# One or two one-element memsets on GpSimd behind each gather, in four stretches of a graph kernel

## The chip, the cores and the metric

The kernel runs on one core of one Trainium2 chip. The metric is the time of one execution on the device in microseconds (us); runs are summed up by their median. The engines are TensorE (PE in the profile, its weight loads PEld), VectorE (DVE), ScalarE (ACT), GpSimd (POOL) and SyncE (SP, which issues most plain DMAs). A profiled execution gives a row for each instruction.

## The reference

12500 nodes with 128 features each and 200000 edges, which are sorted by their target node. Each edge has one of ten relations, the place of the greatest of ten of its attributes. Two layers of the same form follow each other, and then a residual and a normalization:

```python
def _rgcn_layer(x, src, dst, edge_type, w_rel, root, bias):
    N = x.shape[0]
    seg = dst * NUM_REL + edge_type
    xs = x[src]
    sums = jax.ops.segment_sum(xs, seg, num_segments=N * NUM_REL)
    cnt = jax.ops.segment_sum(jnp.ones(seg.shape, x.dtype), seg, num_segments=N * NUM_REL)
    mean = (sums / jnp.maximum(cnt, 1.0)[:, None]).reshape(N, NUM_REL, -1)
    return jnp.einsum('nrd,rdo->no', mean, w_rel) + x @ root + bias

edge_type = jnp.argmax(msg[:, NODE_EMB_DIM:-NODE_EMB_DIM], axis=1).astype(jnp.int32)
h = jax.nn.relu(_rgcn_layer(x, src, dst, edge_type, w_rel1, root1, b1))
g = _rgcn_layer(h, src, dst, edge_type, w_rel2, root2, b2)
out = _layernorm(x + g, axis=-1)
```

All of it is in 32-bit floats.

## The kernel before, in words

The edges are cut into 1563 tiles of 128. For a tile the kernel fetches the 128 source rows with one indirect DMA from GpSimd, which the text calls a gather (`gathered`, line 835; the tile `g`). VectorE builds a one-hot matrix from the targets and relations of the tile's edges, weighted by one over the count (`hots`, line 842; the tile `oh`). TensorE multiplies the two into a bank of PSUM (line 1079 in the first layer, `zp`; line 1620 in the second, `zy` and `zq`), and VectorE adds the bank to the sums of the nodes (line 868 in the first layer, line 1650 in the second; both are named `cc` in the profile).

The first layer (`layer_1`) walks over the tiles in parts of four. The first 177 tiles gather rows of `x`. The other 1386 gather from a table `XH` that holds the input features and, for nodes already done, the first layer's result beside them, 1 KB a row; from these the kernel takes sums for both layers at once. When a block of nodes is complete (`finish`), it is multiplied by the weights of the relations, made into the hidden features, and stored into `XH` and into `YD`, a table of the hidden features times each weight of the second layer.

The second layer (`layer_2`) has two kinds of tiles. 177 of them gather from `YD` for the tiles that had no second half in the first layer (named `YD,idxE`). Then 678 tiles gather from `YD` along a list that is put together on the chip: the edges whose source was not yet known when they were passed (named `YD,idxB`). Between them TensorE multiplies the second layer's stored sums by the weights (line 1533, `alone`), and complete blocks are transposed, added to `x`, normalized and stored (lines 1552 and 775).

Both layers follow an order that is written out by hand, instruction by instruction (`manual_schedule`); each engine works through its own list in order and waits for others by semaphores. On GpSimd this list holds, after some set-up, nothing but gathers: 177 + 1386 + 177 + 678 = 2418. They write into a few buffers in turn, sixteen gathers' worth. Within a buffer the places are filled forwards and backwards by turns, so that in the main the first gather of a group of four carries the wait for TensorE's last reader:

```python
turn = used[id(g)] = 1 - used.get(id(g), 1)
slot = [p % 2 * QB + j if plain else 2 * (QB - 1 - j if turn else j) for j in range(n)]
```

The tile `lane` is a constant of 128 x 128 floats; after lines 361 to 363, which build another constant from it, the kernel does not use it.

Of the kernel before, what the change touches and what calls it, by code (L numbers as in the profile page):

```python
# [31 lines left out]
OB = 7  # L32
GQ = 8
GB2 = 8
AHEAD = 1
BEHIND = 2
LAND = 2
# [33 lines left out]
def rgcn_resnorm_kernel(ctx: ExitStack, tc: tile.TileContext, x, src, dst, attr, w_rel1, root1, b1,  # L71
# [7 lines left out]
    nc = tc.nc  # L79
# [82 lines left out]
    for l, (a, last) in enumerate(((0, SPLIT), (SPLIT, NR))):  # L162
        while a < last:
            b = a + 1
# [9 lines left out]
            a = b  # L174
# [87 lines left out]
    def chunk_rows(c):  # L262
        return min(CT, NT - c * CT)
# [65 lines left out]
    lane = const.tile([P, P], F32, name="lane")  # L329
# [26 lines left out]
    eps = const.tile([P, 1], F32, name="eps")  # L356
    nc.vector.memset(eps, EPS)

    own = const.tile([P, P], F32, name="own")
    first = float(chunk_rows(NCH - 1) * P) - 0.5  # L360
    nc.vector.tensor_scalar(own, lane, first + HALF, None, op0=ALU.is_gt)
# [471 lines left out]
    def gathered(g, j, table, idx, n):  # L833

        nc.gpsimd.indirect_dma_start(out=g[:, j * C:(j + n) * C], out_offset=None, in_=table,  # L835
                                     in_offset=bass.IndirectOffsetOnAxis(ap=idx, axis=0))

    def hots(keys, weights, cols, n, m):

        oh = next_of("oh", hots_)  # L840
        for j in range(n):
            nc.vector.tensor_scalar(oh[:, j * m:(j + 1) * m], cols[:, :m], keys[:, j:j + 1], weights[:, j:j + 1],  # L842
                                    op0=ALU.is_equal, op1=ALU.mult)
        return oh

    def offsets(row, t0, n, limits, ring=True):

        lims = [limits(t0 + j) for j in range(n)]
        if ring:
            laps = [lap_of_tile(t0 + j) * RN for j in range(n)]  # L850
            lims = [(lo - a, hi - a) for (lo, hi), a in zip(lims, laps)]
            assert all(hi + WN <= RW for _, hi in lims)
        vals = nc.values_load_multi_w_load_instructions(  # L853
            row, engines=[DVE], min_val=min(a for a, _ in lims), max_val=max(b for _, b in lims),
            skip_runtime_bounds_check_because="clamped to these nodes on the chip")[1]
        return [nc.s_assert_within(v, a, b, skip_runtime_bounds_check_because="clamped to these nodes on the chip")
                for v, (a, b) in zip(vals, lims)]
# [50 lines left out]
    def layer_1():  # L908
# [135 lines left out]
        fixed = [ps_z.tile([P, YB], F32, name=f"zp{i}") for i in range(4)]  # L1044
        for p in range(-AHEAD, NPT + BEHIND):
            if p + AHEAD < NPT:
                t0, n = parts[p + AHEAD]
                ohs[p + AHEAD] = hots(keyE[:, t0:t0 + n], wE[:, t0:t0 + n], iotaP, n, KW)
            if p < 0:
                continue  # L1050
            t = p * QB
            if p < NPT:
                t0, n = parts[p]
                plain = t0 + n <= NX
                if not plain or p % 2 == 0:
                    g = next_of("g", gathers if plain else gathers[:NEAR])
                if not plain:
                    turn = used[id(g)] = 1 - used.get(id(g), 1)
                slot = [p % 2 * QB + j if plain else 2 * (QB - 1 - j if turn else j) for j in range(n)]
                for j in range(n):  # L1060
                    i = t0 + j
                    idx = idxE[:, i:i + 1]
                    if i < NX:
                        gathered(g, slot[j], x, idx, 1)
                    else:
                        gathered(g, slot[j], XH[:N + limit_of(i)], idx, 2)
                made = (g, ohs.pop(p), slot)
# [67 lines left out]
    for a in range(0, NREL * RW, YB):  # L1135
        m = min(NREL * RW - a, YB)
# [284 lines left out]
    def layer_2():  # L1421
# [156 lines left out]
        for p in range(-AH, NB + BE):  # L1578
# [21 lines left out]
            if p < NB:  # L1600
                second, t0, n, w = bunches[p]
                oh = ohs.pop(p)
                zps[p] = zp = next_of("zp", banks)
                for j in range(n):
                    if made % QB == 0:
                        m = made // QB % NEAR
                        g, first = gathers[m // 2], m % 2 * QB
                        turn = used_[m] = 1 - used_.get(m, 1)
                    at = first + (QB - 1 - made % QB if turn else made % QB)
                    made += 1  # L1610
                    t = t0 + j
                    if second:
                        gathered(g, at, YD[:, :], idxB[:, t:t + 1], 1)
                    else:
                        gathered(g, at, YD[:NREL * (limit_of(t) + 1), :] if t >= T0 else YD[:, :], idxE[:, t:t + 1], 1)
                    gs[j] = g, at
                for j in range(n):
                    g, at = gs.pop(j)
                    o = 0 if second else j * w
                    nc.tensor.matmul(zp[:, o:o + w], g[:, at * C:(at + 1) * C], oh[:, j * w:(j + 1) * w],  # L1620
                                     start=not second or j == 0, stop=not second or j == n - 1)
                    between.run(issued[p] + j + 1)
                i = issued[p + 1]
# [11 lines left out]
            for q in [q for q in sorted(zps) if q <= p - (1 if p >= NB - 4 else BE)]:  # L1635
                second, t0, n, w = bunches[q]
                for j in range(1 if second else n):
                    t = t0 + j
                    if (second, t) not in offs:
                        if second:  # L1640
                            m = min(GB2, (UX if t < UX else NT2) - t)
                            assert {t // P, (t + m - 1) // P} <= ready
                            vals = offsets(rowB[:, t:t + m], t, m, bounds2, False)
                        else:
                            m = min(GB2, (NX if t >= T0 else T0) - t)
                            vals = offsets(rowP[:, t:t + m], t, m, bounds, False)
# [181 lines left out]
```

## Time and profile before

| | |
|---|---|
| Runs | 3640.88 us median of 3 (3640.8 to 3644.05) |
| Profiled execution | 3672.03 us, its span 3670.2 us |
| Granted TensorE clock | 0.753 on average |
| GpSimd | 2287.4 us busy (62%), 2418 gathers of 0.945 us |
| DMA | 529.25 MB, mean 144 GB/s |

A row of a timeline gives the start, the duration, the engine, the line, the operation and the tiles (written <- read), how many instructions the row merges, and in brackets the idle time of the engine before it with what ended it. "issue" is idle time in which the profile shows no wait; "remote" is a wait whose end the profile can't give to an instruction. A row of a group gives busy time and mean duration, then the idle time before the group's instructions, and what ended most of it. Ends of matmuls are modelled. The profiled execution is some 31 us longer than the median of the runs.

### The profile page before, as it was taken

The page shows a single profiled execution, that of the slowest core. Times are in us where ns is not written, and L with a number is a line of the kernel's source. Part 1 is how long each engine was busy: PE and PEld are TensorE (multiplying, and loading weights), DVE is VectorE, ACT ScalarE, POOL GpSimd, SP SyncE. Part 2 cuts the span into 40 slices and gives each one's busy share as a digit, 9 for nine tenths or more (in the row PEclk, how much of TensorE's full clock was granted, in tenths as well). Part 3 has the DMA queues.
Part 4 walks back from the last instruction along what each step waited for, and adds up shares of the span by engine and source line. Part 5 has one row for each costly group of instructions (what it writes and reads, how often), then busy time and mean ns, then how long its engine had stood idle before and what let it go on. Part 6 is the DMA issues. An engine that isn't in the chain of part 4 may idle for free. (4 is left out here: it accounts for less than half of the span.)

```text
span 3670.2 us, 37654 instructions
## 1 busy us (share of the span) xinstructions
PE 2319.0 (63%) x10645; PEld 1779.5 (48%) x10645; DVE 1991.3 (54%) x6410; ACT 511.8 (14%) x799; POOL 2287.4 (62%) x2430
## 2 busy tenths in 40 slices
PE   1557676767676767677666767653566666566444
PEld 0445565555555555565555655543534343333333
DVE  4646476767575757565655656358644232332332
ACT  1111111212121212121212121110000000000000
POOL 5663666666666666666666666556666666666665
PEclk7677787888887888878888878765667777677555
DMA  4553555455555555555555555542334443443222
GB/s 121 159 164 94 187 157 186 151 167 159 177 174 159 189 158 190 158 192 159 190 156 188 159 159 156 147 111 55 105 112 139 129 153 123 148 152 116 61 57 52
DMA packets 345316, 529.25 MB, mean 144 GB/s; under 512 B 55520, under 2 KB 225723, under 8 KB 345100
## 3 DMA queue, kind: packets, MB, share of 16 engines
q0 software_dynamic: 99552, 249.45, 23.9%
q1 hardware_dynamic: 218105, 264.48, 21.7%
q10 hardware_dynamic: 27443, 12.82, 1.2%
q8 instruction: 89, 1.46, 0.2%
q14 instruction: 127, 1.04, 0.1%
HBM read 372.75 MB, written 160.19 MB: 145 GB/s over the span
## 5 line engine op out<-in xcount | busy, mean ns | idle before, releaser
L835 POOL DMA_INDIRECT g<-XH,idxE x1386 | 1309.9, 945 | 769.7 <-issue 368.6
L1079 PEld LDWEIGHTS zp<-oh,g 128*128 128x128 f32 x5898 | 918.4, 234 | 396.5 <-DVE cc L868 180.1
L1079 PE MATMUL zp<-oh,g 128*128 128x120 f32 x5898 | 957.0, 320 | 228.6 <-DVE cc L868 132.3
L868 DVE TENSOR_TENSOR cc<-cc,zp 128x240 f32 (+1 forms) x1563 | 606.5, 388 | 816.1 <-remote 354.1
L835 POOL DMA_INDIRECT g<-YD,idxB x678 | 640.3, 944 | 342.4 <-issue 190.7
L936 PE MATMUL yb<-w,a 128*128 128x512 f32 (+1 forms) x576 | 354.9, 706 | 383.3 <-ACT ys L942 229.0
L842 DVE TENSOR_SCALAR oh<-bank,keyE,wE 128x120 f32<-128x120 f32 x1563 | 517.3, 393 | 0.0
L1620 PEld LDWEIGHTS zy<-oh,g 128*128 128x128 f32 x1168 | 244.8, 275 | 317.9 <-DVE cc L1650 119.1
L1620 PE MATMUL zy<-oh,g 128*128 128x12 f32 (+30 forms) x1168 | 258.4, 347 | 206.5 <-DVE cc L1650 114.6
L942 ACT ACTIVATE ys<-yb 128x512 f32<-128x512 f32 (+2 forms) x291 | 152.8, 525 | 1384.8 <-remote 612.0
L1533 PE MATMUL alone<-cc,w 128*128 128x512 f32 (+1 forms) x440 | 305.3, 782 | 31.6 <-issue 16.9
L936 PEld LDWEIGHTS yb<-w,a 128*128 128x128 f32 x576 | 111.0, 240 | 413.7 <-ACT ys L942 255.9
L828 PE MATMUL pf<-cc,w 128*128 128x256 f32 (+2 forms) x1040 | 254.9, 401 | 25.7 <-issue 13.4
L835 POOL DMA_INDIRECT g<-in_x_dram,idxE x177 | 167.3, 945 | 138.2 <-PE zp L1079 60.0
L828 PEld LDWEIGHTS pf<-cc,w 128*128 128x128 f32 x1040 | 208.4, 215 | 63.9 <-issue 26.0
L835 POOL DMA_INDIRECT g<-YD,idxE x177 | 168.2, 951 | 110.8 <-issue 62.7
L775 DVE TENSOR_TENSOR cc<-pf,x 128x256 f32<-128x256 f32 (+2 forms) x52 | 21.2, 409 | 358.9 <-remote 219.9
L797 ACT ACTIVATE cc<-zero 128x1280 f32<-128x1280 f32 x170 | 214.6, 1262 | 0.0
L1620 PEld LDWEIGHTS zq<-oh,g 128*128 128x128 f32 x542 | 110.8, 253 | 151.2 <-DMA g<-YD,idxB 74.0
L842 DVE TENSOR_SCALAR oh<-columns,keyB,wB 128x45 f32<-128x45 f32 (+35 forms) x678 | 176.8, 335 | 0.0
L1620 PE MATMUL zq<-oh,g 128*128 128x45 f32 (+33 forms) x542 | 122.9, 341 | 84.3 <-DMA g<-YD,idxB 59.5
L1650 DVE TENSOR_TENSOR cc<-cc,zy 128x12 f32 (+24 forms) x306 | 59.0, 193 | 142.6 <-remote 61.0
(265 smaller groups left out, 1528.4 us busy)
## 6 DMA issues: line engine op xcount, KB each, us to landing
cc<-SD SPq DMA_DIRECT2D x21, 2560.0 KB
SD<-cc SPq DMA_DIRECT2D x41, 1280.0 KB
YD<-ys SPq DMA_DIRECT2D x194, 256.0 KB
m<-in_edge_attr_dram SPq DMA_DIRECT2D x48, 672.0 KB
g<-XH,idxE POOLq DMA_INDIRECT x1386
YD<-ys SPq DMA_DIRECT2D x97, 128.0 KB
XH<-hb SPq DMA_DIRECT2D x44, 256.0 KB
g<-YD,idxB POOLq DMA_INDIRECT x678
```

Source lines behind the costliest of these rows:

```text
L775: nc.vector.tensor_tensor(v[:p, s], pr[:p, s], xb[:p, s], op=ALU.add)
L797: nc.scalar.activation(cc[:, l, h * H:(h + 1) * H, o:o + n], zero[:, None, :n].to_broadcast([P, H, n]), AF.Copy)
L828: nc.tensor.matmul(po[:, :n], wsb[l][:, r, :], sums[:, r], start=(r == 0), stop=(w is None and r == NREL - 1))
L835: nc.gpsimd.indirect_dma_start(out=g[:, j * C:(j + n) * C], out_offset=None, in_=table, in_offset=bass.IndirectOffsetOnAxis(ap=idx, axis=0))
L842: nc.vector.tensor_scalar(oh[:, j * m:(j + 1) * m], cols[:, :m], keys[:, j:j + 1], weights[:, j:j + 1], op0=ALU.is_equal, op1=ALU.mult)
L868: nc.vector.tensor_tensor(s, s, z, op=ALU.add)
L936: nc.tensor.matmul(yb[:h, :m], fin_a[k][:, b * P:b * P + h], wsb[1][:, r:r + m // C, :], start=True, stop=True)
L942: nc.scalar.activation(ys[:h, :m], yb[:h, :m], AF.Copy)
L1079: nc.tensor.matmul(zp[:, o + l * KW:o + (l + 1) * KW], g[:, (slot[j] + l) * C:(slot[j] + l + 1) * C], oh[:, j * KW:(j + 1) * KW], start=Tr ...
L1533: nc.tensor.matmul(po[:, :n], wsb[1][:, r, :], sds[j][:, r, :n], start=(r == 0), stop=(r == NREL - 1))
L1620: nc.tensor.matmul(zp[:, o:o + w], g[:, at * C:(at + 1) * C], oh[:, j * w:(j + 1) * w], start=not second or j == 0, stop=not second or j = ...
L1650: nc.vector.tensor_tensor(s, s, zps[q][:, j * w:(j + 1) * w], op=ALU.add)
```

## The change

A table of four stretches is added, in numbers of the gather in the order in which the program issues them, with one or two memsets for each gather of the stretch. The memset writes zero to one element of `lane`. A counter of gathers runs along while the program is built. Gathers 400 to 799 and 1740 to 1999 get one memset each, gathers 800 to 1199 and 2000 to 2199 get two; all others get none. Numbers 400 to 1199 lie in the first layer (all of them gathers from `XH`); number 1740 is the first gather along the list that is put together on the chip.

```diff
+SPACED = ((400, 800, 1), (800, 1200, 2), (1740, 2000, 1), (2000, 2200, 2))
...
+    pause = lane[:1, :1]
+    number = [0]
...
         nc.gpsimd.indirect_dma_start(out=g[:, j * C:(j + n) * C], out_offset=None, in_=table,
                                      in_offset=bass.IndirectOffsetOnAxis(ap=idx, axis=0))
+        for a, b, m in SPACED:
+            if a <= number[0] < b:
+                for _ in range(m):
+                    nc.gpsimd.memset(pause, 0.0)
+        number[0] += 1
```

## The prediction

> **What bounds the kernel now.** I read the page first (engine shares), then the gathers' rows in the four stretches that get memsets, then the order of time inside a few runs of gathers.
>
> ```profile
> span 3670.2 us, 37654 instructions
> ...
> PE 2319.0 (63%) x10645; PEld 1779.5 (48%) x10645; DVE 1991.3 (54%) x6410; ACT 511.8 (14%) x799; POOL 2287.4 (62%) x2430
> ```
>
> No engine is full: each of them waits more than a third of the time. So the question is what a gather waits for. Gathers are numbered from 0 in the order in which they are issued. Numbers 400, 800 and 1200 start at 645.46, 1246.88 and 1836.99 us, numbers 1740, 2000 and 2200 at 2666.74, 3050.01 and 3336.52 us; these starts cut out the four stretches. In the table by stage (stretch, its length, busy time and count of line 835) and in the groups of GpSimd in the same four windows (busy, mean ns | idle before, and what ended it):
>
> ```profile
> 645.46:1246.88 601.42, 378.18 (x400) 0.82 0.54 168
> 1246.88:1836.99 590.11, 377.96 (x400) 0.83 0.55 174
> 2666.74:3050.01 383.27, 245.67 (x260) 0.74 0.41 130
> 3050.01:3336.52 286.51, 188.87 (x200) 0.73 0.47 148
> ...
> L835 POOL DMA_INDIRECT g<-XH,idxE x400 | 378.2, 945 | 221.3 <-issue 107.4 <-remote 54.3 <-PE zp L1079 49.9
> L835 POOL DMA_INDIRECT g<-XH,idxE x400 | 378.0, 945 | 213.1 <-issue 107.7 <-remote 53.2 <-PE zp L1079 42.3
> L835 POOL DMA_INDIRECT g<-YD,idxB x260 | 245.7, 945 | 137.6 <-issue 71.2 <-remote 34.6 <-PE zy L1620 21.7
> L835 POOL DMA_INDIRECT g<-YD,idxB x200 | 188.9, 944 | 97.6 <-issue 55.5 <-remote 28.1 <-PE zq L1620 8.0
> ```
>
> A gather keeps GpSimd 0.945 us, and the next one starts 0.30 us after it even when nothing is waited for (rows below): 1.25 us from start to start. The stretches take 1.50, 1.48, 1.47 and 1.43 us per gather (length by count). The rest is waiting. With 0.30 us per gather taken off the idle time, it is 221.3 - 120 = 101.3, 213.1 - 120 = 93.1, 137.6 - 78 = 59.6 and 97.6 - 60 = 37.6 us, or 0.253, 0.233, 0.229 and 0.188 us per gather. That is the room into which the memsets go.
>
> How the room lies is seen in order of time. Twelve gathers of the first layer and sixteen of the second, each with the wait that closes the run (last number in the brackets: idle before):
>
> ```profile
> 1199.46 0.95 POOL L835 DMA_INDIRECT g<-XH,idxE  x1 [2.33 <-PE zp L1079]
> ...
> 1217.30 0.94 POOL L835 DMA_INDIRECT g<-XH,idxE  x1 [3.15 <-PE zp L1079]
> 1218.55 0.94 POOL L835 DMA_INDIRECT g<-XH,idxE  x1 [0.30 <-issue]
> ...
> 1231.05 0.95 POOL L835 DMA_INDIRECT g<-XH,idxE  x1 [0.30 <-issue]
> 1234.85 0.95 POOL L835 DMA_INDIRECT g<-XH,idxE  x1 [2.86 <-remote]
> ...
> 2806.01 0.94 POOL L835 DMA_INDIRECT g<-YD,idxB  x1 [3.32 <-PE zy L1620]
> ...
> 2824.80 0.95 POOL L835 DMA_INDIRECT g<-YD,idxB  x1 [0.30 <-issue]
> 2829.07 0.94 POOL L835 DMA_INDIRECT g<-YD,idxB  x1 [3.32 <-remote]
> ```
>
> So GpSimd runs a dozen gathers or so at 1.25 us, stops at the head of a group of four until TensorE has given a buffer back (2.9 to 3.3 us here, the usual 0.30 us included), and runs again: 17.55 us for the twelve, 23.06 us for the sixteen.
>
> The trace holds a small version of the change. Two runs of the same lengths contain a pause of their own (0.81 and 0.52 us where 0.30 is usual):
>
> ```profile
> 1152.03 0.95 POOL L835 DMA_INDIRECT g<-XH,idxE  x1 [1.37 <-PE pf L953]
> ...
> 1162.53 0.94 POOL L835 DMA_INDIRECT g<-XH,idxE  x1 [0.81 <-issue]
> ...
> 1169.76 0.94 POOL L835 DMA_INDIRECT g<-XH,idxE  x1 [2.54 <-PE zp L1079]
> ...
> 2728.19 0.94 POOL L835 DMA_INDIRECT g<-YD,idxB  x1 [2.74 <-PE zy L1620]
> ...
> 2743.43 0.94 POOL L835 DMA_INDIRECT g<-YD,idxB  x1 [0.52 <-issue]
> ...
> 2751.25 0.94 POOL L835 DMA_INDIRECT g<-YD,idxB  x1 [3.14 <-remote]
> ```
>
> With 0.51 us more inside the run the closing wait is 2.54 us, not 2.86 to 3.15, and twelve gathers take 17.73 us against 17.55 (and 17.84 for the run that starts at 1199.46). With 0.22 us more, sixteen take 23.06 us: the same. Time lost inside a run is taken off the wait at its end. What is behind that wait sets the pace, not GpSimd.
>
> **The change part by part.** It adds 400 x 1 + 400 x 2 + 260 x 1 + 200 x 2 = 1860 memsets of one element to GpSimd's queue, each behind a gather and ahead of the next; nothing is removed or moved, no DMA is added, no other engine reads what they write. The line that names the element and the counter cost nothing on the chip: they act while the program is built. A memset's target was last used by VectorE before the first gather, so its wait, if it has one, has long been met; behind it stands the next gather alone, and who waits for that is TensorE.
>
> What one memset costs behind a gather no row shows. The nearest are the memsets with which the program begins:
>
> ```profile
> 0.25 0.10 POOL L1816 MEMSET const-float32-0.0<- 128x1 f32 x1 [0.25 <-issue]
> 0.28 0.10 POOL L1816 MEMSET const-float32-1.0<- 128x1 f32 x1
> 0.31 0.11 POOL L1816 MEMSET const-bfloat16-1.0<- 128x1 bf16 x1
> ```
>
> One lasts 0.10 us, and the next starts 0.03 us behind it. Lower end: nothing (it fits in the 0.30 us gap), or 0.03 us each, 56 us in all. Upper end: the 0.30 us gap comes once more for each, 0.40 us each, 744 us. I take 0.10 us for a memset alone and 0.13 us for a pair (the second 0.03 us behind the first), the rows of the same instruction on the same engine: 40, 52, 26 and 26 us in the four stretches, 144 us in all.
>
> The Trainium skill, Perfetto Trace Analysis, "GPSIMD Engine Instruction", says to time such instructions by the spacing of their starts, not by the span reported; by that rule and the rows above the estimate is 0.03 us each, 12, 24, 8 and 12 us, and the forecast would be the same.
>
> What of the 144 us lies on the path: they stand against 101.3, 93.1, 59.6 and 37.6 us of room, so each stretch has room over, and by the runs with a pause the wait at the end of the run gives it back. Sum: 0 us. If the cover goes, the cost is the surplus per stretch. The break-even is 0.25 us for the single memset in the first stretch and 0.23 us in the third, 0.233 and 0.188 us for the pair in the second and fourth. The fourth is the thinnest, also because there TensorE does wait for gathers: the first fence lists who waited for line 835 in the first stretch, after the dots in the fourth.
>
> ```profile
>   PE yb L936: 14.6, 2
>   PE pf L953: 1.2, 1
> ...
>   PE zy L1620: 19.5, 16
>   PEld zq L1620: 17.7, 19
> ...
>   PE zq L1620: 12.3, 16
> ```
>
> In the first layer 16 us of 601 are waited for gathers; in the fourth stretch about 32 us of 287 on TensorE (19.5 + 12.3). Late gathers there matter only if the run's end no longer absorbs them.
>
> **The rivals.** *Faster: the pauses let signals through.* Late in a run VectorE, ScalarE and GpSimd start together long after TensorE's last matmul; after the last gather of the program a consumer starts at once:
>
> ```profile
> 1506.74 1.05 PE L1079 MATMUL zp<-oh,g 128*128 128x120 f32 x8
> 1512.84 0.84 DVE L868 TENSOR_TENSOR cc<-cc,zp 128x240 f32 x2 [3.47 <-remote]
> 1512.88 0.60 ACT L942 ACTIVATE ys<-yb 128x512 f32<-128x512 f32 x1 [8.38 <-remote]
> 1513.07 0.94 POOL L835 DMA_INDIRECT g<-XH,idxE  x1 [2.13 <-remote]
> ...
> 3655.61 0.45 PE L1552 MATMUL pf<-ident,cc 128*128 128x128 f32 x1 [3.75 <-DVE cc L1650]
> 3656.09 0.29 DVE L775 TENSOR_TENSOR cc<-pf,x 128x128 f32<-128x128 f32 x1 [0.63 <-PE pf L1552]
> ```
>
> From TensorE's end to the others' start it is 1512.84 - 1507.79 = 5.05 us in a run, 0.03 us without gathers. If back-to-back gathers hold TensorE's signals up and a pause frees them, all closing waits could go. At 1.35 and 1.45 us per gather (0.10 us for one, 0.20 for two) the stretches would take 540 + 580 + 351 + 290 = 1761 us against 1861.3: 100 us less at most, 3541 us. Half of it, since TensorE and VectorE have limits of their own: 3590 us. Against it: the pauses of 0.51 and 0.22 us above shortened nothing.
>
> *Slower: a pair costs more than its room.* One mechanism: each memset holds GpSimd for its full time and the second waits for the first. At 0.15 us each the second stretch lacks 120 - 93.1 = 27 us and the fourth 60 - 37.6 = 22 us, the singles nothing: + 49 us, 3690 us. It decides from 0.094 us per memset in the fourth stretch, 0.117 us in the second. For it: 0.10 us is already the row's length. Far end: 0.40 us each against the room lacks 59 + 227 + 44 + 122 = 452 us, 4093 us.
>
> *Slower: nothing is absorbed.* If the closing wait is counted from GpSimd's last gather of a run, every memset adds: 56 us (0.03 each) to 186 us (0.10 each), 3697 to 3827 us. Against it stand the same two runs.
>
> *Slower: the shared port.* VectorE's one-hot rows in the third and fourth stretch take 120.4 us of 669.8 (second row: the gathers of the third stretch, shortest, median and longest in ns):
>
> ```profile
> L842 DVE TENSOR_SCALAR oh<-columns,keyB,wB 128x46 f32<-128x46 f32 (+25 forms) x460 | 120.4, 334 | 0.0
> ...
> L835 POOL DMA_INDIRECT g<-YD,idxB x260: 938/944/1022, 2666.7 to 3048.8; - x130
> ```
>
> A memset that met one of these would wait half of 0.334 us in 18% of cases, 0.03 us on average: 12 us for the 400 memsets of the fourth stretch. With 0.20 us a pair there (40 us) that makes 52 against 37.6: + 14 us, 3655 us. Against it: the longest gather is 78 ns over the median. The Trainium skill, SBUF — State Buffer, "Who interferes with whom", has it that VectorE in a two-port mode and a GpSimd instruction lock each other out of a shared port; no run here shows that wait.
>
> **How the numbers follow.** The profiled execution took 3672.03 us (span 3670.2), 31 us above the median of the runs, 3640.88; I carry differences over to the median. A change under 0.2% (7 us) can't be told from none here.
> - Absorbed, no change: 0.38, 3641 us, with a range of its own from 3633 to 3648.
> - Signals pass, faster: 0.32, about 3590 us, 3541 at most.
> - A pair costs more than its room: 0.15, about 3690 us; with the far end of 0.40 us: 0.05.
> - Nothing absorbed: 0.06, 3697 us and more. The port: 0.04, 3655 us.
>
> The forecast is the likeliest, 3641 us. The range from 3580 to 3695 leaves out the deep half of the faster case's tail (about 0.08) and the far slower cases (about 0.12). Faster 0.32, same 0.38, slower 0.30.
>
> **What would show it.** Right: 1860 memsets on GpSimd's row; start to start 1.28 to 1.35 us with one, 1.28 to 1.4 us with two; closing waits shorter by that much, and the four stretches still about 601, 590, 383 and 287 us long. Wrong to the slow side: a start to start of over 1.44 us with two, no closing waits left, and TensorE's waits for gathers up. Wrong to the fast side: VectorE's and ScalarE's starts follow TensorE within 0.1 us in mid-run, and stretches shorter by tens of us. A stretch without memsets that moves by more than 5 us would be something I have not seen.

## The result, and the profile after

The changed kernel takes 3650.7 us (median) beside 3640.84 us of the kernel before: a ratio of 1.0037, interval 1.0020 to 1.0055, so 7 to 20 us more (the ratio is not that of the two medians, 1.0027; the two can differ by some 0.1%). That is slower by a little, inside the range of 3580 to 3695 us, but outside the 3633 to 3648 us of the case that I held likeliest. The profiled execution took 3649.4 us, at its median; that of before stood 31 us above its own.

Page of the kernel after (span, busy time by engine):

```profile
span 3647.6 us, 39514 instructions
...
PE 2315.0 (63%) x10645; PEld 1770.1 (49%) x10645; DVE 1994.4 (55%) x6410; ACT 512.0 (14%) x799; POOL 2451.8 (67%) x4290
```

4290 - 2430 = 1860 instructions more on GpSimd. The same four stretches (gathers 400, 800, 1740 and 2000 onward) of the kernel after, by windows with GpSimd's busy time in line 838 alone:

```profile
636.55:1234.01 597.46, 378.24 (x401) 0.81 0.54 169
1234.01:1826.18 592.17, 377.87 (x401) 0.82 0.56 173
2649.68:3026.70 377.02, 246.00 (x261) 0.74 0.42 133
3026.70:3321.46 294.76, 188.77 (x201) 0.76 0.46 144
```

Against before (601.42, 590.11, 383.27, 286.51) the singles' stretches are not longer; the pairs' are, the second by 2 us, which is within the spread shown further down, the fourth by 8 us. The parts without memsets are shorter by 8.9, 6.3 and 7.5 us (up to gather 400, 1200 to 1740, from 2200 on), since before's profiled execution was a long one; so single stretches of these two traces are no fair comparison, and further traces are added below. What a memset does is seen in order of time, GpSimd of the kernel after, first in the third stretch (one), then in the fourth (two):

```profile
2702.18 0.94 POOL L838 DMA_INDIRECT g<-YD,idxB  x1 [2.44 <-remote]
2703.13 0.09 POOL L843 MEMSET lane<- 1x1 f32 x1
2703.43 0.94 POOL L838 DMA_INDIRECT g<-YD,idxB  x1 [0.22 <-issue]
2704.38 0.09 POOL L843 MEMSET lane<- 1x1 f32 x1
2704.68 0.94 POOL L838 DMA_INDIRECT g<-YD,idxB  x1 [0.21 <-issue]
...
3103.46 0.94 POOL L838 DMA_INDIRECT g<-YD,idxB  x1 [0.61 <-issue]
3104.40 0.23 POOL L843 MEMSET lane<- 1x1 f32 x2
3104.79 0.94 POOL L838 DMA_INDIRECT g<-YD,idxB  x1 [0.15 <-issue]
3105.73 0.23 POOL L843 MEMSET lane<- 1x1 f32 x2
3106.11 0.94 POOL L838 DMA_INDIRECT g<-YD,idxB  x1
3107.06 0.23 POOL L843 MEMSET lane<- 1x1 f32 x2
3107.44 0.94 POOL L838 DMA_INDIRECT g<-YD,idxB  x1
3108.39 0.23 POOL L843 MEMSET lane<- 1x1 f32 x2
3109.23 0.94 POOL L838 DMA_INDIRECT g<-YD,idxB  x1 [0.61 <-issue]
```

One memset disappears in the 0.30 us gap: 1.25 us from start to start (2703.43 to 2704.68), as without it. A pair makes it 1.33 us (3103.46 to 3104.79), and once per four gathers 1.79 us (3107.44 to 3109.23): a group of four takes 5.77 us, 1.44 us per gather, with no wait for another engine. That is as much as the fourth stretch had in all. The two memsets of a pair do not overlap: one lasts 0.09 us, the two 0.23 us, so the second starts 0.15 us after the first and 0.06 us after its end (medians of all 600 pairs). In the trace each memset waits for a semaphore that the memset before it raises; both write the same element. The waits fit the slower pace. Who waited for line 838 in the fourth stretch after (the rows of before are in the prediction), then VectorE's waits there, before and after:

```profile
  PEld zy L1628: 70.7, 64
  PE zy L1628: 55.6, 47
  PEld zq L1628: 42.3, 42
  PE zq L1628: 35.5, 30
```

```profile
DVE cc L1650 <- remote: 50.6, 7, 16.3
DVE cc L775 <- remote: 43.4, 4, 15.5
```

```profile
DVE cc L778 <- PE pf L1560: 87.6, 10, 12.7
DVE cc L1658 <- PE zy L1628: 32.2, 14, 5.4
```

TensorE's waits for gathers went from 31.8 to 91.1 us (zy and zq); VectorE's largest waits of before, without a releaser that the profile can name ("remote", the late signals), are gone from this stretch. GpSimd has become the bound of that stretch.

### The profile page after: what moved, and what is told of

Its sections match the earlier page's. It is cut to its first block, busy times and chain, and to the rows that moved or that the text cites. A ratio compares the mean times of both kernels' runs of the same rounds, so it can differ in the third digit from the quotient of the medians.

```text
span 3647.6 us, 39514 instructions
## 1 busy us (share of the span) xinstructions
PE 2315.0 (63%) x10645; PEld 1770.1 (49%) x10645; DVE 1994.4 (55%) x6410; ACT 512.0 (14%) x799; POOL 2451.8 (67%) x4290
## 5 line engine op out<-in xcount | busy, mean ns | idle before, releaser
L1087 PEld LDWEIGHTS zp<-oh,g 128*128 128x128 f32 x5898 | 902.6, 230 | 428.0 <-DVE cc L876 210.8
L843 POOL MEMSET lane<- 1x1 f32 x1860 | 167.3, 90 | 35.4
```

The costliest lines, as they stand in the source:

```text
L843: nc.gpsimd.memset(pause, 0.0)
L1087: nc.tensor.matmul(zp[:, o + l * KW:o + (l + 1) * KW], g[:, (slot[j] + l) * C:(slot[j] + l + 1) * C], oh[:, j * KW:(j + 1) * KW], start=Tr ...
```

## The experiments

Theory, formed from these rows: one memset is free; a pair makes GpSimd's own pace 1.44 us per gather and a little over, of which 0.46 us per group falls on the group's head; a stretch takes the slower of that pace and of what the other engines allow. Rivals: the loss comes from the number of instructions, from every pair, or is the time of the memsets. On two chips the kernel before took 3096 to 3098 us, on a third 3636 to 3640 us. Each kernel is compared with before on its own chip. The first eight ran where before takes 3096 us, the last four where it takes 3640 us.

**One memset behind every gather.**

```
SPACED = ((0, 2418, 1),)
```

> One memset behind each of the 2418 gathers, none a pair. Theory 'price at the head of a group' (in the changed kernel one memset hides in the 0.30 us gap, start to start still 1.25 us; a pair makes it 1.33 us, and 1.79 us at the head of each group of four gathers): no change, 3641 us, within 6; start to start stays 1.25 us, closing waits as before. Rival 'each instruction costs' (the 10 us come from 1860 more instructions, 5.4 ns each, wherever they stand): 3654 us.

Measured: 3110.75 us against 3096.33, 1.0047 (1.0033 to 1.0061), 14 us for 2418 memsets, 0.006 us each. Start to start stays 1.25 us. On this evidence alone "each instruction costs" fits; the next runs refute it.

**Pairs in one layer.**

```
SPACED = ((177, 1563, 2),)      # first layer
SPACED = ((1563, 2418, 2),)     # second layer
```

> Two memsets behind each of the 1386 gathers of the first layer, none elsewhere. Theory 'price at the head': GpSimd's own pace there becomes (3 x 1.33 + 1.79) / 4 = 1.445 us per gather, under the 1.51 us (2088 us for 1386) that the stretch takes: no loss, 3635 to 3647 us; long closing waits gone, and VectorE's waits for late signals much reduced. Rival 'each instruction costs': 3656 us. Rival 'every pair adds its 0.08 us' (nothing absorbed): 3641 + 111 = 3752 us.

> Two memsets behind each of the 855 gathers of the second layer, none elsewhere. Theory 'price at the head': GpSimd's own pace, 1.445 us per gather, is over the 1.433 us that the fourth stretch had, and TensorE waits for gathers as it does in the changed kernel's fourth stretch (1.474 us against 1.433 us): 855 x 0.041 = 35 us, 3676 us (3660 to 3690). Rival 'each instruction costs': 3650 us. Rival 'every pair adds its 0.08 us': 3709 us.

Measured: 3379.77 and 3260.74 us, 1.0917 (1.0902 to 1.0932) and 1.0537 (1.0523 to 1.0551): 283 and 164 us more, 0.20 and 0.19 us per pair. None of my numbers held; they supposed that before takes 3641 us. The group's 5.77 us less four times 1.25, divided by four, is 0.19 us, about this price.

**Where in the group the price falls.** Pairs in the second layer, left out behind the last gather of each group; then there alone:

```
-            if a <= number[0] < b:
+            if a <= number[0] < b and number[0] % 4 != 2:   # and in the other run == 2
```

> As the run with pairs in the second layer, but nothing behind the last gather of each group of four, so that no memset stands right ahead of a group's head. Theory 'price at the head': the 0.46 us per group goes, GpSimd's own pace is (3 x 1.33 + 1.25) / 4 = 1.31 us, and the loss goes with it: 3641 us (3625 to 3648). If the pauses let TensorE's signals through as well, it may be below 3630. Rival 'every memset costs', by number or by time: three quarters of the loss of the run with all pairs, 3667 us if that one is 3676.

> Second layer alone: two memsets behind the last gather of each group of four, so right ahead of the next group's head; nothing behind the other three. Where the kernel before takes 3096 us (no closing waits, GpSimd sets the pace): theory 'price at the head' 0.54 us per group (1.79 - 1.25), 214 groups: +116 us, or +108 by subtraction (164 us with all pairs less 56 without those at the head). Rival 'the delay gathers up over several pairs in a row' (a single pair is no more than its 0.08 us): +17 us. Where the kernel before takes 3641 us (closing waits of 0.23 us per gather, 0.92 us per group): both theories within 0.5% of 3641 us, and below if a pause per group frees the late signals (GpSimd's own pace is 1.385 us per gather against 1.43: up to 38 us less).

Measured: 3152.37 us against 3096.33, 1.0183 (1.0169 to 1.0197), 56 us; and 3205.83 against 3098.48, 1.0347 (1.0333 to 1.0361), 107 us. The parts add up: 56 + 107 = 163, all pairs 164. The 642 pairs away from a head cost 0.09 us each, the 213 at a head 0.50 us, close to the +108 us that I expected by subtraction. "Every memset costs alike" would have put 123 us on the first. The expected 0 there supposed room that this chip does not have.

**One long memset in place of the pair.**

```
SPACED = ((1563, 2418, 1),)
-                    nc.gpsimd.memset(pause, 0.0)
+                    nc.gpsimd.memset(lane, 0.0)     # 128x128
```

> Second layer alone: one memset of 128x128 elements behind each gather (0.204 us by the row of such a memset at the program's start) in place of the pair, so about the time of a pair (0.23 us from the first's start to the second's end) in one instruction. Theory 'the price at the head is one of number, a second instruction behind the gather keeps the head from being prepared early': start to start 1.33 to 1.37 us for all four gathers of a group, no 1.79 us; where the kernel before takes 3096 us +68 to +103 us, against +164 with pairs. Rival 'it is one of time': as with pairs, about +164 us. Where the kernel before takes 3641 us: no change within 8 us by the first theory, +35 us by the second.

GpSimd in order of time with the long memset, then with the pair at the head alone:

```profile
2801.84 0.95 POOL L838 DMA_INDIRECT g<-YD,idxB  x1 [0.17 <-issue]
2802.80 0.22 POOL L843 MEMSET lane<- 128x128 f32 x1
2803.18 0.95 POOL L838 DMA_INDIRECT g<-YD,idxB  x1 [0.17 <-issue]
```

```profile
2806.01 0.95 POOL L838 DMA_INDIRECT g<-YD,idxB  x1 [0.30 <-issue]
2806.96 0.23 POOL L843 MEMSET lane<- 1x1 f32 x2
2807.81 0.94 POOL L838 DMA_INDIRECT g<-YD,idxB  x1 [0.62 <-issue]
```

Measured: 3171.89 us, 1.0234 (1.0220 to 1.0248), 73 us against the pair's 164, within the +68 to +103 us of the first theory. About as long as the pair (0.22 beside 0.23 us), but 1.34 us nearly everywhere and no price at the head. So 0.46 us is a matter of the second instruction, not of time. What the traces show of it (medians of 167 heads): with one memset the semaphore instruction of a group's head starts 0.18 us before the gather ahead of it does, with the long one 0.12 us before; with a pair it starts 1.07 us after that gather's start, about when the second memset does, and the head's gather starts 0.72 us behind it. That this lost lead is the cause is read from the order, not tried. Nor was a rival tried: the second memset of a pair also waits for the first, which wrote the same element. Whether the price is one of number or of this wait, a pair that writes two separate tiles would have to tell.

**The changed kernel, and the one before, on such a chip.**

> The changed kernel itself. Where the kernel before takes 3096 us: 600 gathers with a pair at (283 + 164) / 2241 = 0.20 us each, 660 with one memset at 14.4 / 2418 = 0.006 us: +124 us, 3220 us (1.040). Rival 'the memsets cost the same on every chip': +10 us. Where it takes 3641 us: 3651 us (1.0037) again.

> The kernel before, for its trace beside the others of this chip. Where it takes 3096 us: start to start 1.25 us nearly throughout, no closing waits, and VectorE starts within 0.05 us of TensorE's end. Where it takes 3641 us: closing waits of 0.2 us per gather and VectorE's late starts, as in the first trace.

Measured: 3236.41 us against 3098.48, 1.0447 (1.0433 to 1.0461), 138 us where the first chip shows 10, and 14 more than I expected. The trace of before is of an execution of 3104.51 us. Windows of the four stretches, before and then changed, on this chip:

```profile
520.00:1024.20 504.20, 379.33 (x401) 0.88 0.64 200
1024.20:1525.40 501.20, 379.28 (x400) 0.88 0.65 205
2236.80:2562.70 325.90, 246.62 (x261) 0.78 0.51 162
2562.70:2812.90 250.20, 189.23 (x200) 0.77 0.50 159
```

```profile
516.00:1023.60 507.60, 379.45 (x400) 0.87 0.64 199
1023.60:1611.20 587.60, 378.83 (x400) 0.85 0.57 175
2318.20:2646.40 328.20, 246.73 (x260) 0.79 0.51 161
2646.40:2941.20 294.80, 189.54 (x201) 0.75 0.43 135
```

Before takes 1.25 to 1.26 us per gather here: GpSimd hardly ever waits, there is no room. With pairs the fourth stretch takes 294.80 us, and 294.76 us on the first chip: the same pace on both, so there GpSimd alone sets it. The second takes 587.60 us against 592.17. Why the room is missing, GpSimd in order of time and VectorE's waits in the whole kernel before, on this chip:

```profile
1460.28 0.95 POOL L835 DMA_INDIRECT g<-XH,idxE  x1 [0.30 <-issue]
1461.53 0.95 POOL L835 DMA_INDIRECT g<-XH,idxE  x1 [0.30 <-issue]
1462.79 0.95 POOL L835 DMA_INDIRECT g<-XH,idxE  x1 [0.30 <-issue]
```

```profile
DVE cc L775 <- PE pf L1552: 296.3, 49, 11.0
DVE cc L868 <- PE zp L1079: 285.6, 149, 8.4
```

No "remote" stands among the waits; on the first chip it was the longest:

```profile
DVE cc L868 <- remote: 354.1, 112, 7.4
DVE cc L868 <- PE zp L1079: 239.5, 73, 11.3
```

The median time from the end of the last matmul to the start of a VectorE sum (line 868 or 1650) that had been idle for over 0.15 us is 0.037 or 0.038 us in the four stretches here, and 0.51, 0.37, 0.35 and 0.43 us on the first chip. So the late signals, and with them the closing waits and the room, went with the chip; what makes the chips differ, these runs don't show.

**More matmuls, without and with pairs.** These runs met the chip with late signals.

```
-                    for l in (0, 1) if i >= NX else (0,):
+                    for l in (0, 0, 1) if 400 <= i < 1200 else (0, 1) if i >= NX else (0,):
SPACED = ()                      # the first
SPACED = ((400, 1200, 2),)       # the second
```

> No memset at all; in the tiles 400 to 1199 of the first layer the first product of each tile is issued twice (same operands, same result), 800 more matmuls of some 0.31 us. It is there to make room beside GpSimd, to be read with the next run. Where the kernel before takes 3096 us: TensorE has 1.04 of 1.25 us per gather now, so the 800 gathers should take 1.4 to 1.55 us each and not 1.25: 3096 + 120 to 240 us. Where it takes 3641 us: up to +80 us.

> The same added matmuls, and two memsets behind each of the gathers 400 to 1199. Theory 'the slower of two paces sets the time' (a pair makes GpSimd's own pace 1.47 us per gather, and costs only what that is over the pace that the rest allows): time above the run with the matmuls alone is 800 x (1.47 - its pace), nothing where its pace is 1.47 or more, 56 us where it is 1.40. Rival 'a pair always adds its 0.22 us': 800 x 0.216 = +173 us over it, whatever its pace.

Measured: 3658.59 and 3664.21 us against 3635.99, 1.0057 (1.0041 to 1.0074) and 1.0069 (1.0052 to 1.0086). Windows of the two stretches, GpSimd in line 838, matmuls alone and then with pairs:

```profile
643.00:1244.80 601.80, 378.97 (x401) 0.88 0.54 168
1244.80:1836.50 591.70, 378.88 (x400) 0.89 0.55 173
```

```profile
643.80:1245.40 601.60, 377.85 (x400) 0.90 0.54 168
1245.40:1843.10 597.70, 377.77 (x401) 0.91 0.55 172
```

800 pairs cost 0 and 6 us here, 173 by the price of the other chips: absorbed, the rival is refuted. The stretches went at 1.50 and 1.48 us per gather, just over the pairs' 1.47. The added matmuls made less room than I meant them to: TensorE's busy time rose from 416 and 409 to 492 us in each, 1.23 us per gather. Against before's trace on the first chip (601.42 and 590.11) the stretches did not grow, but that execution was a long one; against the only trace of this chip that has neither memsets nor added matmuls there, that of the last run below (592.4 and 583.3), they grew by 9 and 8 us, most of the 22 us.

**Pairs away from the heads, both layers.**

```
SPACED = ((177, 2418, 2),)
+ and number[0] % 4 != (3 if number[0] < 1563 else 2)
```

> Pairs behind three of every four gathers from number 177 to the end, none right ahead of a group's head: GpSimd's own pace is 1.31 to 1.33 us. Where the kernel before takes 3096 us: 2241 gathers at 56 / 855 = 0.0655 us, +147 us, 3243 us. Where it takes 3641 us, theory 'pauses of 0.08 us do not free the late signals': 3641 us within 10; rival 'they do': down to 1.35 us per gather where 1.5 stand, 3400 us or less.

Measured: 3658.23 us, 1.0055 (1.0034 to 1.0075): 12 to 27 us more, where I had expected no more than 10. Some 1680 pairs at 0.09 us are about 150 us of GpSimd's time, so most is absorbed, but not all, though 1.33 us is well under the pace of 1.48. VectorE's waits on this run, first line, show that these pauses freed nothing (354.1 before, 375.0 in the last run below, which has no memsets in the first layer):

```profile
DVE cc L876 <- remote: 393.0, 107, 8.3
```

What the rest of some 20 us is, the runs don't settle.

**Pairs in the second layer, on the chip with late signals.**

> Two memsets behind each of the 855 gathers of the second layer, as in the third run, for a chip on which the kernel before takes about 3640 us. Theory 'the slower of two paces': GpSimd's own pace with a pair is 1.474 us per gather there (294.8 us for the 200 of the fourth stretch, on a chip of either kind), the rest allows 1.43 to 1.45, so TensorE waits for gathers: +20 to +40 us. Rival 'fully absorbed': no change. Rival 'nothing absorbed': +164 us as measured where the kernel before takes 3096 us. Where it takes 3096 us again: +164 us.

Measured: 3648.76 us against 3639.76, 1.0018 (1.0003 to 1.0033), 1 to 12 us, less than the 20 to 40 that I expected. The layer's last 1280.1 us (from gather 1563 to the end) equal the 1278.5 of the same kernel on the other kind of chip, so the pairs' pace does bind; but without pairs in the layer the layer takes 1273.1, 1271.3 and 1266.2 us (before, and the two kernels with more matmuls), on average 10 less. I had carried one stretch's difference, 0.041 us per gather, over the whole layer; the layer's first 177 gathers and the 260 from 1740 on were slower than that stretch and had more room (8 us less and 3 more than in those three traces on average); the fourth stretch and the end cost 7 and 8 us.

The run shows one thing more. VectorE's longest waits in the second layer, in the kernel before and then here (line 778 is line 775 of before):

```profile
DVE cc L775 <- remote: 219.9, 16, 23.7
```

```profile
DVE cc L778 <- PE pf L1560: 322.5, 41, 12.8
```

From gather 1563 on, VectorE's waits that end in "remote" fall from 377 to 10 us, and from gather 1740 on its sums start 0.038 us (median) after the last matmul, as on the other chips. So pairs behind every gather, the heads included, do end the late signals of the second layer on this chip; pairs away from the heads did not. Whether the longer pause at the head does it, or that GpSimd is now the slowest, was not tried. Nothing is won by it, since GpSimd's own pace then sets the time.

No version that ran beats the kernel before on its chip.

## Why the prediction was right or wrong

Lengths of the stretches on the chips with late signals (us, from the starts of the gathers at their ends; without memsets: before, and the stretches of the later runs that hold neither memsets nor more matmuls):

```
gathers      without memsets        mean   changed  difference  pairs' pace alone
400- 800     601.4 592.4           596.9   597.5     +0.6
800-1200     590.1 583.3           586.7   592.2     +5.5       587.6
1740-2000    383.3 376.9 379.0     379.7   377.0     -2.7
2000-2200    286.5 289.2 286.8     287.5   294.8     +7.3       294.8
```

Together +10.7, beside 9.9 by the medians and 13 by the ratio. The single differences are no surer than the spread of some 9, 7, 6 and 3 us within a row; the fourth alone is clear of it.

- The room, 0.253, 0.233, 0.229 and 0.188 us per gather, and that the fourth stretch is the thinnest: right. A delay inside a run comes off the closing wait: right in the main, by the 0 and 6 us for 800 pairs beside 173 us elsewhere.
- The price of a memset: wrong in both directions, and this is the step that failed: the term of the sum was mis-sized. One costs 0 (the lower end, "it fits in the gap"), not 0.10; a pair costs (587.6 - 501.2) / 400 = 0.216 us in the first layer and (294.8 - 250.2) / 200 = 0.223 us in the second, not 0.13. I had priced it by duration and spacing of the first memsets, which carry no wait and start 0.03 us apart; the second of a pair waits for the first and starts 0.15 us after it, although I wrote that a memset's wait has long been met. And I had no row for what stands behind the second one, the head of the group. That the 144 us of my pricing come near the measured 131 us (86.4 + 44.6) is luck: the two errors nearly cancel. By my own break-even (0.233 and 0.188 us for the pair) the measured price gives nothing in the second stretch and 44.6 - 37.6 = +7 us in the fourth. The right price in the same sum would have given 3648 us.
- So the rival "a pair costs more than its room" came true, with the place and threshold that it names (0.094 us per memset in the fourth stretch, measured 0.11), not with its figure of 0.15 each. Of its mechanism the half is right that the second memset waits for the first; most of the price falls at the head of a group, of which it says nothing.
- What would show it: start to start 1.25 us with one (I said 1.28 to 1.35); with two 1.33, within 1.28 to 1.4, but 1.79 at the heads. The sign that I gave for the slow side, over 1.44 us with two and TensorE's waits up, is there in the fourth stretch: 1.47 us and 91.1 us. The last sign, a stretch without memsets that moves by more than 5 us, came too (6 to 9 us shorter), and says no more than that before's profiled execution was a long one.
- "Signals pass": pauses of 0.08 us away from the heads freed nothing. Pairs behind every gather did free the signals, in the fourth stretch ("remote" from 103 to 0 us) and in the whole second layer of the last run, but GpSimd's slower pace took all of that time.
- "Nothing is absorbed" is what happens on the other chips, +138 us, because the late signals and with them the room are absent there. From one chip's trace I could not see that the room goes with the chip.
- The Trainium skill, Perfetto Trace Analysis, "GPSIMD Engine Instruction" (time by the spacing of starts): the trace agrees for the single, whose 0.09 us of busy time add nothing to the spacing of the gathers; my 0.03 us from it was wrong for the pair. The port: the Trainium skill, SBUF — State Buffer, "Who interferes with whom", has it that VectorE in a two-port mode and a GpSimd instruction lock each other out. In the fourth stretch the median memset took 88 ns, the longest 199, and the mean gather 944 as before: no loss of a size that counts here.

## What to carry to other kernels

Price an instruction put between others by the spacing of what follows it, at each place in the pattern: a gap may hide the first, and the second may cost several times its length at one place of the pattern. Idle time absorbs a delay up to its own size per stretch, so compare the new pace of the engine with the pace of the stretch, not its busy time with the span. And ask whether the idle time is the program's or comes and goes with the chip: the same change cost 0.4% on one chip and 4.5% on another.

## What was not expected of the hardware

- The same program takes 3096 to 3098 us on two chips and 3636 to 3641 us where the first result and the last four runs were taken, 17.5% more, with equal durations of a gather (0.945 to 0.949 us). The difference shows as the start of VectorE's sums 0.04 us or 0.35 to 0.51 us after TensorE's last end (medians of the four stretches); why is open.
- With one memset behind every gather, where before takes 3096 us, a stall of 0.3 to 1.9 us beyond the usual spacing comes every 106 gathers in both layers (ahead of gathers 431, 537 and so on to 1491, and of 1809, 1915, 2021, 2127, 2233 and 2339), and none at these places without memsets. These 17 stalls are 14.2 us together, all of the 14 us that this run is longer: the 0.006 us of a single are theirs. They stand at the same gathers with pairs, so they go by the count of gathers, not of memsets; their cause is open.
- 800 more products on TensorE in two stretches raised the granted clock there from 0.82 and 0.83 to 0.88 and 0.89, with the stretches at 601.8 and 591.7 us.
